# Early combine scores computed token-major, with the queries as the stationary side, in a decoder layer kernel

## The chip, the cores and the metric

The kernel runs on one core of a Trainium2 chip. The metric is the device time of one execution in microseconds (us), as the median of several runs. Three runs of the kernel before gave 1522.98, 1519.18 and 1523.01 us. Shorter is better.

## What is computed

One decoder layer on x of shape (2, 2048, 512) in fp32: a state-space mixer, a cross-attention to 77 context tokens and a soft mixture of 16 experts, each with a residual and a layer norm behind it. The last part is the one that matters here. Sixteen slots attend to all tokens (dispatch), each expert works on its slot, and the tokens then attend to the slots (combine), with 16 heads of 32 features:

```python
o = q + _mha(q, x, x, d_Wq, d_bq, ...)             # slots gather from tokens
h = _layernorm(os, e_ln_g, e_ln_b)
u = silu(h @ e_W1 + e_b1); g = silu(h @ e_Wg + e_bg)   # one expert per slot
o = o + ((u * g) @ e_W2 + e_b2)
out = _mha(x, o, o, c_Wq, c_bq, ...)               # tokens gather from slots
# in _mha: scores = einsum(qh, kh) / sqrt(32); softmax over the keys
x = _layernorm(x + out)
```

The combine's softmax runs over 16 slots for each of 4096 tokens and 16 heads.

## The kernel before

The kernel has four stages: in-projection and scan, token mixing with cross-attention and dispatch, the experts, and the combine. The first two end near 930 us and the change doesn't touch them.

**Experts** (`expert`, L1159). The 16 experts run one after the other on 32 rows (2 sequences, 16 slots). The weights of an expert are 12 MB, in 12 blocks of 1 MB: four of `e_W1`, four of `e_Wg`, four of `e_W2`. SP issues their loads in order, into a ring of slabs (`weights`, L1047); a load waits until PE has read what its slab held. PE multiplies a block of W1 or Wg into `up`; the block's 512 columns go to four column strips of 32. At k = 0 the bias is added by four more products with `bb`. ACT takes Silu of `up` into `sv`, DVE multiplies the two into `ag`, PE transposes `ag` into `tp` (L1181, PSUM tag `tr`), DVE copies the expert's columns into `aT` (L1185), and PE adds the four W2 blocks into `yac` (L1189).

**Work beside the experts.** While the weights of experts 2 to 13 stream, PE computes the combine's queries `Qc`, features on the partitions (`queries`, L1214). Behind expert 13 the slots of the first 14 experts are final: `slots_now`, `slot_heads` and `by_heads` (L1265 to L1292) make their keys and lay them out block-diagonally over the four heads of a group in `bd["c_Wk"]` (in the trace `c_Wkd`).

**Early scores** (`early`, L1315). The scores of all tokens against the 14 finished slots are computed while experts 14 and 15 run. A group g has 512 tokens, and there are 8 groups. In a group, PE makes the scores with the slots on the partitions (L1325, stationary `c_Wkd`, 64 columns, moving 512 query columns) into two PSUM tiles `lp` (in the trace `mm`), ACT copies them to `es`, and PE transposes them in pieces of 128 tokens into `sc` (L1333, in the trace `tr<-cst,es`), so that tokens are on the partitions. For each half group (256 tokens) DVE takes the maximum (L1338), subtracts it (L1339), ACT takes the exponential (L1341), and DVE sums (L1342). The result stays in `p`, one tile for each half group.

**What sets their order.** `early` is a generator. `beat` (L1149) is called behind each of the 12 weight blocks of experts 14 and 15, and takes the next steps from it; the steps are dealt over the first `b1` beats. What a beat takes may not be issued before the beat's last product. Steps that are left at the end are taken behind the last expert (L1350). Within these bounds a scheduler of the framework places the instructions in each engine's queue when the program is built. The PSUM tag `tr` has two buffers, shared by `sc`, `tp` and the transposes of the queries.

**Combine** (L1360 on). The last slots are completed (`slots_now` into `ysb`, `yp`, `oT`), their keys and values made (`fo`, `kr`, `ftr`, `bdl`), the scores of the last two slots added (`fsc`), the weights scaled (`factors`, `attend`), multiplied by values and output weights (`finish`), normed and stored.

Of the kernel before, what the change touches and what calls it, by code (L numbers as in the profile page):

```python
# [25 lines left out]
# columns of the packed per-partition vectors  # L26
# [3 lines left out]
# columns of the packed shape constants  # L30
# [34 lines left out]
def merge(*flows):  # L65
    """Emit flows side by side, each given as (generator, steps), at the pace that ends them together."""
    todo = [[f, n, 0] for f, n in flows]
    while todo:
        f = min(todo, key=lambda t: t[2] / t[1])
        f[2] += 1  # L70
        try:
            next(f[0])
        except StopIteration:
            todo.remove(f)


def weave(flows, depth, lag):
    """Emit `depth` flows side by side; the next one starts `lag` steps after the last."""
    flows = list(flows)
    live, since = [], lag  # L80
    while flows or live:
        if flows and len(live) < depth and (since >= lag or not live):
            live.append(flows.pop(0))
            since = 0
        since += 1
        for f in list(live):
            try:
                next(f)
            except StopIteration:
                live.remove(f)  # L90
# [123 lines left out]
 'b1': 18,  # L214
# [9 lines left out]
def tile_decoder(ctx, tc, a, out, dbg=None, upto=9, opt=None):  # L224
# [68 lines left out]
    with ExitStack() as st:  # L293
        class Pools:
            """tiles by tag from pools of their own, so that the next phase takes over each pool's room as it falls free"""
# [33 lines left out]
        def first_operands():  # L329
            """the first tokens and the weights in the order of their use, in pieces"""  # L330
            xt = sb.tile([128, 4, TB], FP, tag="xt", bufs=1, name="xt")
            xh = sb.tile([128, 4, TB], FR, tag="xh", bufs=2, name="xh")
            xl = sb.tile([128, 4, TB], FR, tag="xl", bufs=2, name="xl")
            nc.sync.dma_start(xt, a["xT"][0][:, 0:TB].rearrange("(k p) t -> p k t", p=128))
            wr = {}
            for q in (1, 0, 2):
                wr[q] = big_tile("wr", [128, 4, D], "CS" if q == 0 else "BS")
                for k in (0, 2):
                    nc.sync.dma_start(wr[q][:, k:k + 2, :], rows_of("wi")[:, k:k + 2, q * D:q * D + D])
            nc.sync.dma_start(cst, a["cst"])  # L340
            for k in (0, 2):
                split(xh[:, k:k + 2], xl[:, k:k + 2], xt[:, k:k + 2])
            x0.extend((xh, xl))
            for q in (1, 0, 2):
                for k in range(4):
                    split(wi[q][0][:, k, :], wi[q][1][:, k, :], wr[q][:, k, :], engs[EA.get("fl%d%d" % (q, k), 1)], EA.get("fh%d%d" % (q, k), 0))
                    if q != 1 and k % 2:
                        ready_.add(("wi", q, k))
                        yield
                if q == 1:  # L350
                    yield

        # decay: dt, cumulative sums, normalisers in rows (section of 512 tokens, head)
# [59 lines left out]
        def setup():  # L413
            """operands of the next phase from weights, a half at a time"""
# [5 lines left out]
            # cross-attention keys and values  # L420
# [32 lines left out]
            # dispatch queries folded with the key weights  # L453
# [91 lines left out]
        def scan_loads(c):  # L545
            """operands of one pass that holds the three hi/lo products of the 32 state rows"""
            scr = cvs[c // 2][1]
            sl = slice((c % 2) * 128, (c % 2) * 128 + 128)
            BS = big_tile("BS", [128, 4, 4, 128], "BS", FR)
            CS = big_tile("CS", [128, 4, 4, 128], "CS", FR)  # L550
            for q in range(3):
                dq = slice(32 * q, 32 * q + 32)
                for t, nm, j in ((BS, "Bc", q % 2), (CS, "C", q // 2)):
                    (nc.sync, nc.scalar)[EA.get("bq" if nm == "Bc" else "cq", 0)].dma_start(t[dq].rearrange("p g r t -> p (g r) t").bitcast(FP),
                                      scr[nm][j][:, sl].rearrange("(h n) t -> n h t", n=32).bitcast(FP))
            return BS, CS
# [3 lines left out]
        def scan_ready(c):  # L560
            """token-major x (weighted) and B of a chunk"""
# [79 lines left out]
        def next_weights():  # L641
            """weights of the next phase, into the room that the in-projection's leave"""
# [8 lines left out]
        def spread(*flows):  # L651
            """names side by side, each given as (name, steps), at the pace that ends them together"""
            return "".join(n for _, _, n in sorted(((k + 1) / n, i, c) for i, (c, n) in enumerate(flows) for k in range(n)))
# [30 lines left out]
    def stats(pool_, z, p=128, tg=""):  # L684
        """mean and 1/std over the free axis of z [p, 512]; the latter from exp(-ln(var+eps)/2) and a Newton step"""
# [13 lines left out]
    with ExitStack() as st:  # L699
# [222 lines left out]
        # Two half periods of four quarters for every tile; a stage works on the tile `back` periods ago.  # L922
        # Each quarter holds one group of heads of the attention and one block of products.
# [5 lines left out]
        def period(p):  # L929
            """operations of one period, in the order of their issue"""  # L930
# [86 lines left out]
    if True:  # L1017
# [17 lines left out]
        # the combine's weights stay in the slabs 0, 1, 2: the keys' come before the last experts', the others after  # L1035
# [34 lines left out]
        # sums over the tokens, divided by the sums of the weights, with their features on the partitions  # L1070
# [20 lines left out]
        # the slots after the dispatch and their norm; feature 4p+j sits on partition p  # L1091
# [17 lines left out]
        def mean(v):  # L1109
            """mean over the features, on all partitions"""  # L1110
            part = sb.tile([128, 32], FP, tag="part", bufs=2, name="part")
            dve.tensor_reduce(part, v.rearrange("p j b s -> p (b s) j"), AX.X, ALU.add)
            mp = ps.tile([128, 32], FP, tag="mm", bufs=2, name="mp")
            mm(mp, mean_w, part, True, True)
            return mp
# [27 lines left out]
    Qc = []  # L1143
    if True:
# [4 lines left out]
        def beat(e, at):  # L1149
            """scores of the tokens in the waits for the last expert's weights"""  # L1150
            if e >= NE - NL:
                n = tail["n"] = tail.get("n", -1) + 1
                b0, b1 = opt.get("b0", 0), opt.get("b1", 22)
                k = [max(0, min(1, (i - b0) / (b1 - b0))) * 3 * NT for i in (n, n + 1)]
# [101 lines left out]
        # what the slots hold besides the experts' sums  # L1256
# [8 lines left out]
        def slots_now(on):  # L1265
            """the slots with what the experts gave so far"""
# [8 lines left out]
        def slot_heads(nm, on, PS, pool_, tags=("kr0", "kr1")):  # L1275
            """keys or values of the slots without their bias, features on the partitions"""
# [11 lines left out]
        def by_heads(dst, src, cv, n):  # L1288
            """block-diagonal over the heads of a group"""
# [14 lines left out]
        esp = ctx.enter_context(tc.tile_pool(name="es", bufs=1, side="left", reuse_waits="tile"))  # L1304
# [10 lines left out]
        def early():  # L1315
            """the scores of all slots but the last experts': maxima, exponentials and their sums"""
            for g in range(B * NT // 2):
# [3 lines left out]
                es = [esp.tile([128, 512], FP, tag=f"es{m}", bufs=1, name="es") for m in range(2)]  # L1321
                for m in range(2):
                    lp = PE_("mm", (128, 512))
                    for q in range(2):
                        mm(lp[64 * q:64 * q + 64, :], bd["c_Wk"][:, 2 * m + q, b].rearrange("p r s -> p (r s)"),  # L1325
                           Qc[b][:, 2 * m + q, t0:t0 + 512], True, True)
                    cp(opt.get("ese%d" % m, 0), es[m], lp)
                yield
                for h in range(2):
                    sc = PE_("tr", (128, 2, 16, 16))  # L1330
                    for t in range(2):
                        for m in range(2):
                            pe.transpose(sc[:, t, 8 * m:8 * m + 8, :].rearrange("p h s -> p (h s)"),  # L1333
                                         es[m][:, (2 * h + t) * 128:(2 * h + t) * 128 + 128], ident)
# [26 lines left out]
    with ExitStack() as st:  # L1361
# [18 lines left out]
        def slot_outputs(b, m):  # L1380
            """values of the slots times the output weights for two groups of heads"""
# [4 lines left out]
        def split_outputs(b, m):  # L1386
            vp = vps.pop((b, m))
            if m == 0:
                # the weights of a head sum to one, so that its rows carry the output bias
# [3 lines left out]
        # keys of the last slots, each group of heads on the first columns of a strip  # L1393
# [12 lines left out]
        def last_slots(g):  # L1406
            """scores of 512 tokens for the last slots"""
# [8 lines left out]
        def factors(g):  # L1416
            """factors for the weights of the other slots, and the weights of the last ones"""
# [175 lines left out]
```

## Time and profile before

| What | us |
|---|---|
| Time, median of 3 runs (lowest, highest) | 1522.98 (1519.18, 1523.01) |
| Span of the profiled execution | 1526.7 |
| PE, DVE, ACT, POOL busy in it | 1372.1, 905.6, 616.3, 446.2 |
| First to last early score product (`mm`, `tr`) | 1378.9 to 1421.5 |
| Last `yac` products | 1428.4 to 1434.3 |
| First scores of the last slots (`fsc`) | 1440.1 |
| Combine behind them, to the end | 1441 to 1526.7 |

The profiled execution is 3.7 us longer than the median of the runs. The page has 40 slices of 38 us; the part that the change touches, 1379 to 1441 us, lies in slices 37 and 38, counted from 1. In the table by stage DVE is busy for 53.5 us of the 56.8 us from 1441.2 to 1498.0, and for 32.4 of the 62.2 us from 1379.0 to 1441.2. An instruction's row names the tile that it writes and those that it reads; a product of fp32 tiles shows twice, once for each of its two passes.

### The profile page before, as it was taken

Reading aid. Unit: us, or ns where it says so; the run is one execution under the profiler, and the core shown is the slowest. Engines: PE = TensorE matmul, PEld = TensorE weight load, DVE = VectorE, ACT = ScalarE, POOL = GpSimd, SP = SyncE. Lnnn points to the kernel's source line nnn. Section 1 sums busy time; section 2 is a strip of 40 time slices with the busy share of each in tenths; the row PEclk is TensorE's granted clock in tenths of the full one; section 3 lists DMA queues with packets and bytes.
Section 4 is the critical chain, followed back from the end, with each engine's and each line's share of the span. In section 5 each row is a group of like instructions: output and inputs, shape, how many; then the busy total and the mean of one; then the engine's idle time right before and its main releaser. Section 6 shows DMA issues by size and latency. Waiting matters only on the chain.

```text
span 1526.7 us, 27382 instructions
## 1 busy us (share of the span) xinstructions
PE 1372.1 (90%) x10282; PEld 996.3 (65%) x10282; DVE 905.6 (59%) x2142; ACT 616.3 (40%) x1683; POOL 446.2 (29%) x496
## 2 busy tenths in 40 slices
PE   7899999978999999999999997948979788889896
PEld 5788889857888888888888875205544445433364
DVE  6897796856788888888888764001211111115597
ACT  5544443524565565665656552001000000104456
POOL 3644543535444444444443321000000000000054
PEclk9999998988999999999999998969989998999998
DMA  9797987895122221311110138898999999999447
GB/s 312 194 214 206 227 219 194 223 248 143 56 56 60 66 63 57 96 57 56 57 53 18 70 139 350 355 415 359 418 419 418 420 419 419 418 421 408 174 149 251
DMA packets 177499, 339.61 MB, mean 222 GB/s; under 512 B 12027, under 2 KB 123131, under 8 KB 152536
## 3 DMA queue, kind: packets, MB, share of 16 engines
q1 hardware_dynamic: 161072, 311.25, 58.5%
q10 hardware_dynamic: 16296, 26.62, 5.1%
q8 instruction: 81, 1.33, 0.4%
q14 instruction: 50, 0.41, 0.1%
HBM read 299.56 MB, written 38.27 MB: 221 GB/s over the span
## 4 chain that ended last, share of the span: by engine, by line
PE 60%; DVE 17%; DMA 15%; ACT 4%; issue 3%; SPq 1%; POOL 1%; ACTq 0%; POOLq 0%; DVEq 0%
PE mm L231 25%; DMA ew<-in_e_W 8%; PE pj L231 7%; PE up L231 7%; DMA ew<-in_e_Wg 5%; PE tr L826 3%; PE yac L231 2%; PE sc L231 2%; PE y L231 2%; PE dps L231 2%; PE uu L231 2%; PE gp L231 1%; DVE X L528 1%; ACT pp L816 1%; PE tr L719 1%
## 5 line engine op out<-in xcount | busy, mean ns | idle before, releaser
L231 PE MATMUL up<-ew,hT 128*32 128x512 f32 x944 | 134.7, 645 | 34.4 <-DMA ew<-in_e_W 30.9
L818 POOL TENSOR_TENSOR pp<-pp,den 128x308 f32<-128x308 f32 x128 | 90.1, 708 | 161.4 <-DVE den L817 109.0
L1174 ACT ACTIVATE sv<-up 128x512 f32<-128x512 f32 x32 | 19.1, 597 | 269.8 <-PE up L231 247.0
L1183 POOL MEMSET aT<- 128x512 f32 x16 | 8.3, 524 | 403.5 <-PE yac L231 401.8
L231 PE MATMUL mm<-xTh,cqh 128*128 128x256 f32 x256 | 76.2, 309 | 26.2 <-ACT xTh L234 26.2
L1233 DVE TENSOR_TENSOR Qc<-mm,vec 128x512 f32<-128x512 f32 x32 | 22.1, 691 | 125.3 <-PE mm L231 125.3
L242 DVE TENSOR_TENSOR xTl<-tr,xTh 128x512 fp32r<-128x512 f32 x32 | 21.3, 687 | 115.1 <-ACT xTh L234 115.0
L231 PEld LDWEIGHTS up<-ew,hT 128*32 128x32 f32 x944 | 26.0, 112 | 96.6 <-issue 56.7
L826 PE MATMUL tr<-cst,pp 128*77 128x128 f32 x512 | 80.6, 282 | 1.4 <-ACT pt L234 1.2
L231 PE MATMUL mm<-x1Th,w30h 128*128 128x256 f32 x256 | 76.9, 301 | 4.4 <-DVE ql L786 3.6
L816 ACT ACTIVATE pp<-sc,mx 128x77 f32<-128x77 f32 x240 | 75.4, 327 | 13.3 <-DVE mx L813 12.5
L234 ACT COPY pt<-tr 77x512 f32<-77x512 f32 x96 | 55.7, 582 | 61.2 <-PE tr L826 34.2
L231 PE MATMUL mm<-xTl,cqh 128*128 128x256 f32 x256 | 78.4, 308 | 1.2 <-DVE xTl L242 1.2
L231 PEld LDWEIGHTS mm<-xTh,cqh 128*128 128x128 f32 x256 | 51.5, 207 | 40.2 <-ACT xTh L234 30.2
L231 PE MATMUL mm<-xTh,cql 128*128 128x256 f32 x256 | 75.2, 296 | 0.0
L231 PE MATMUL mm<-x1Tl,w30h 128*128 128x256 f32 x256 | 74.4, 291 | 0.9 <-DVE x1Tl L722 0.9
L231 PE MATMUL mm<-x1Th,w30l 128*128 128x256 f32 x256 | 73.8, 288 | 0.0
L826 PEld LDWEIGHTS tr<-cst,pp 128*77 128x77 f32 x512 | 59.4, 148 | 16.3 <-issue 11.1
L234 ACT COPY raw<-pj 128x512 f32<-128x512 f32 x48 | 28.1, 584 | 99.1 <-PE pj L231 65.0
L231 PE MATMUL yac<-ew,aT 128*32 128x512 f32 x488 | 61.1, 637 | 7.1 <-issue 4.7
L744 POOL TENSOR_TENSOR ut<-ut,fb 128x512 f32<-128x512 f32 x32 | 41.0, 1282 | 80.4 <-DMA ut<-Ud 40.9
L231 PEld LDWEIGHTS mm<-xTl,cqh 128*128 128x128 f32 x256 | 52.3, 204 | 18.4 <-issue 14.7
(376 smaller groups left out, 4358.1 us busy)
## 6 DMA issues: line engine op xcount, KB each, us to landing
ew<-in_e_W SPq DMA_DIRECT2D x119, 1024.0 KB, 15.9
ew<-in_e_Wg SPq DMA_DIRECT2D x60, 1024.0 KB, 14.1
BS<-scrBc SPq DMA_DIRECT2D x48, 256.0 KB, 5.7
CS<-scrC SPq DMA_DIRECT2D x48, 256.0 KB, 6.2
xt<-in_x SPq DMA_DIRECT2D x32, 256.0 KB, 2.8
ut<-Ud SPq DMA_DIRECT2D x32, 256.0 KB, 3.4
fb<-fd SPq DMA_DIRECT2D x128, 64.0 KB, 3.0
x2d<-x ACTq DMA_DIRECT2D x32, 256.0 KB, 2.0
```

Source lines behind the costliest of these rows:

```text
L231: return pe.matmul(o, lhsT=l, rhs=r, start=start, stop=stop, **kw)
L234: (act.copy, dve.tensor_copy, pool.tensor_copy)[e](o, i)
L242: (lo_eng or dve).tensor_tensor(lo, src, hi, ALU.subtract)
L528: dve.scalar_tensor_tensor(dst, raw[:, j, 1 + t:1 + t + TB], w4[:, t:t + 1], dst, ALU.mult, ALU.add)
L719: pe.transpose(tp[:, k * 128:k * 128 + 128], src[:, k * 128:k * 128 + 128], ident)
L744: (act, dve, pool)[EN.get('uf', 1)].tensor_tensor(ut, ut, fb, ALU.mult)
L816: act.activation(pp[:, r, :], sv[:, r, :], AF.Exp, bias=mx[:, h:h + 1], accum_out=den[:, h:h + 1])
L818: (act, dve, pool)[EN.get('d%d' % hg, 2)].tensor_tensor(pp, pp, den[:, h4].unsqueeze(2).to_broadcast([128, 4, S]), ALU.mult)
L826: pe.transpose(tp[0:S, r * 128:r * 128 + 128], pp[:, r, :], ident)
L1174: last["silu"] = act.activation(sv, up, AF.Silu)
L1183: pool.memset(aT, 0.0)
L1233: dve.tensor_tensor(Qc[b][:, mp * 2:mp * 2 + 2, t1:t1 + TB], qq, vec[:, V_CQ + mp * 2:V_CQ + mp * 2 + 2].unsqueeze(2).to_broadcast([128, 2 ...
```

## The change

In `early` the products change sides. The queries of 128 tokens are now the stationary operand and the block-diagonal keys of a head group, 64 columns, the moving one, so that the scores come out with tokens on the partitions, straight into `sc`. The tiles `lp` and `es`, the ACT copies and the transposes go, and so does the pool of `es`. The four operations behind the scores stay as they are.

A group now yields behind each block of 128 tokens and behind each half group, six times, where it yielded three times. `beat` deals 4 x 8 = 32 steps where it dealt 3 x 8 = 24, over 15 beats where it had 18. Docstrings and comments of the kernel are blanked, and the lines behind `early` have numbers smaller by six.

```diff
- 'b1': 18,
+ 'b1': 15,
...
-                k = [max(0, min(1, (i - b0) / (b1 - b0))) * 3 * NT for i in (n, n + 1)]
+                k = [max(0, min(1, (i - b0) / (b1 - b0))) * 4 * NT for i in (n, n + 1)]
...
-        esp = ctx.enter_context(tc.tile_pool(name="es", bufs=1, side="left", reuse_waits="tile"))
         xrp = ctx.enter_context(tc.tile_pool(name="xrp", bufs=1, side="left", reuse_waits="tile"))
...
-                es = [esp.tile([128, 512], FP, tag=f"es{m}", bufs=1, name="es") for m in range(2)]
-                for m in range(2):
-                    lp = PE_("mm", (128, 512))
-                    for q in range(2):
-                        mm(lp[64 * q:64 * q + 64, :], bd["c_Wk"][:, 2 * m + q, b].rearrange("p r s -> p (r s)"),
-                           Qc[b][:, 2 * m + q, t0:t0 + 512], True, True)
-                    cp(opt.get("ese%d" % m, 0), es[m], lp)
-                yield
                 for h in range(2):
                     sc = PE_("tr", (128, 2, 16, 16))
                     for t in range(2):
-                        for m in range(2):
-                            pe.transpose(sc[:, t, 8 * m:8 * m + 8, :].rearrange("p h s -> p (h s)"),
-                                         es[m][:, (2 * h + t) * 128:(2 * h + t) * 128 + 128], ident)
+                        for hg in range(4):
+                            mm(sc[:, t, 4 * hg:4 * hg + 4, :].rearrange("p r s -> p (r s)"),
+                               Qc[b][:, hg, t0 + (2 * h + t) * 128:t0 + (2 * h + t) * 128 + 128],
+                               bd["c_Wk"][:, hg, b].rearrange("p r s -> p (r s)"), True, True)
+                        yield
```

## The prediction, made before the change was run

> **What bounds the kernel now.** The granted-clock row of the page first: full speed nearly everywhere, so stages can be compared. Then the chain of waits from 1360 us on, because the order of instructions in the two built programs is the same on every engine until the first early score, at 1378.9 us, and again from the combine's first products (`fo`) on. Start and length in us, engine, line:
>
> ```profile
> 1395.86 0.63 PE tp L1181 x4
> 1396.49 0.69 issue
> 1397.18 1.07 PE yac L231 x8
> 1398.24 1.02 PE tr L1333 x8
> 1399.27 1.00 PE yac L231 x8
> 1400.26 1.87 PE mm L231 x8
> ...
> 1424.09 1.28 ACT L1174
> 1425.39 0.61 ACT sv L1174
> 1426.02 0.70 DVE ag L1178
> 1426.85 1.09 PE tp L1181 x4
> 1427.94 0.47 issue
> 1428.41 5.83 PE yac L231 x32
> ```
>
> PE is the bound from 1397 to 1423.4: weights (`up`, `yac`) and scores (`mm`, `tr`) alternate without a hole. Then a Silu table load, Silu, a product and a transpose lead to the last `yac`. In the table by stage the DMA share is 0.98 in 1423.4-1428.4 and 0.07 after: the stream ends near 1429, and as two other matrices (c_Wv, c_Wo; 1 MB each, 2.5 us at 415 GB/s) come behind the last expert's, its own are in by about 1425. DMA is 3 us off the bound. Now the groups that go, and the row nearest to what comes (busy us, mean ns | idle before):
>
> ```profile
> L231 PE MATMUL mm<-Qc,c_Wkd 128*64 128x512 f32 x64 | 16.4, 611 | 0.0
> L1333 PE MATMUL tr<-cst,es 128*128 128x128 f32 x64 | 9.8, 284 | 0.0
> ...
> L231 PE MATMUL kp<-qbd,dwk 128*128 128x64 f32 x32 | 3.9, 271 | 0.0
> ```
>
> The third has the new shape exactly: 128-column stationary side, 64 moving columns, fp32 in two passes, 3.9/32 = 0.122 us a pass; inside a run passes start 0.112 us apart.
>
> Last, stretches of 3.41 us, the step in which the clock changes here (PE, PEld, DVE, ACT, POOL busy, then clock):
>
> ```profile
> 258.62:262.03 3.41, 3.41 (x32) 3.41 (x32) 1.88 (x9) 2.48 (x5) 0.38 (x2) 1.00 0.90 278
> 262.03:265.44 3.41, 3.41 (x19) 3.41 (x17) 2.52 (x6) 0.00 (x0) 1.31 (x1) 0.50 1.02 275
> ...
> 1391.84:1395.25 3.41, 1.70 (x9) 0.61 (x8) 1.92 (x4) 3.37 (x6) 0.00 (x0) 1.00 1.01 420
> ...
> 1422.56:1425.97 3.41, 0.83 (x8) 0.00 (x0) 2.05 (x4) 2.98 (x4) 0.00 (x0) 1.00 0.99 415
> 1425.97:1429.39 3.42, 2.06 (x12) 1.10 (x16) 0.96 (x3) 1.30 (x2) 0.00 (x0) 0.50 0.81 308
> ```
>
> The first row matters most: PE was busy all of it, and yet the next stretch ran at half clock. Half of it was this:
>
> ```profile
> 258.78 1.85 PE L231 MATMUL qp<-sqTs,dwq 128*128 128x16 f32 x16
> ```
>
> 16-column passes wait for their weight loads; the array hardly streams. So what the clock follows looks like streamed columns, not busy time.
>
> **The change part by part.** *Products.* Per 512 tokens, four 512-column products (1.87 us in the chain) and eight transposes (1.02) go, 2.9 us, times 8 = 23.1 us of PE. In come 128 products of two passes: a half-block of 256 tokens (8 products) is 16 x 0.112 = 1.79, with the 0.16 us that a change of kind costs (the eight transposes take 1.02 where 8 x 0.109 = 0.87) 1.95 us, times 16 = 31 us. PE work grows by 8 us; it can't shrink unless a pass undercuts its weight load, which no row shows.
>
> *Copies.* Sixteen ACT copies of 0.58 us go (9.3 us). ACT is idle as long again in the stretch, so worth 0, except that products no longer wait for them. DVE's three operations and ACT's exponential per half-block stay. Pool `es` goes and `xrp` moves; SP's and POOL's orders are unchanged, one early wait less on SP near 990 us: 0.
>
> *Beats.* A group of 512 tokens now has 6 steps, 48 in all, but 32 are spread over 15 beats. So 22 of 32 token blocks are issued in the beats and 10 (5 half-blocks) are flushed behind the last expert. In the built order 8 products stand between its transposes and `yac`, 7 between its four weight blocks, 9 behind them and 16 between `yp` and `fo`.
>
> *Sum at full clock.* I lay the new order out with 1.0 us per weight block, 1.86 with its bias, 1.05 / 1.95 / 3.7 for 4 / 8 / 16 products. From 1378.9: 16 products to 1382.6, then block, 8, block, 8, block to 1389.5, 16 to 1393.2. The transposes `tp` need the PSUM buffer of the fifth half-block, whose subtraction stands on DVE behind `ag` and a sum that waits for an exponential behind Silu and a table load: 1390.3 + 1.28 + 0.6 + 0.6 + 1.15 = 1393.9. `aT` is now behind two more DVE operations, to 1395.4. So `yac` starts at 1395.5 (1397.2 before), PE standing 0.7 + 1.0 us. Then 15 us of the old blocks and 8.8 us of products end the last `up` near 1419.3 (1423.4 before): 4 us won, all weights in. The Silu table is loaded ahead, so `tp` follows after 1.5 us instead of 3.5. `yac` with its interleaved products ends at 1429.4 (1434.3). There DVE takes over: from `ysb` four half-blocks of 1.7-1.9 us, each with its exponential between subtraction and sum, hold `oT` and the first `kr` back to 1438.5 (1437.8), and the combine's `fsc` starts at 1441.2 against 1440.1. All 5 us are given back: **+1 us**. The combine is DVE-bound (53.5 of 56.8 us) in its old order and moves with it.
>
> *The clock.* An fp32 pass of 512 columns lasts 0.43 us, so 64 columns stream 0.053, half of the 0.112 us that the pass takes. Counting streamed time so (fp32r at half of that) over all stretches of 3.41 us at full clock: all 20 with a share up to 0.35 were followed by half clock, all from 0.46 up kept it, 0.38-0.45 went both ways. Of those at half clock, all up to 0.74 stayed and all from 0.78 came back. The score products alone are at 0.46-0.48: just on the safe side until PE stands. Around 1393 it does: 1.4 us of products at 0.46, `tp` (0.43), 1.7 us of nothing give 1.07/3.41 = 0.31; the luckiest position of the stretch gives 0.39. I take the fall.
>
> The rule that speaks against this is in the Trainium skill, TensorE: Matmul & The Clock Gate, "Why this matters for your kernels": the clock is lost only after gaps between matmuls above some 3 us. No gap here is above 1.5, so by the rule the price is 0 and the sum +1. By the row at 258.6, with no gap at all, it falls. I go by the row.
>
> At half clock a weight block takes 1.8 us and 4 / 8 products 2.0 / 3.9. Blocks and products by turns give 0.67-0.72, under the 0.78 that brings it back, until the last expert's first block with its bias (3.6 us of dense streaming). From 1395.5 to there 11.0 us become 20.5: **+9.5 us**. Behind it all moves by that. Then 9 products, the 32-column `yp` and 16 products stand in a row: 0.38, a second fall, whose 2.8 us of products and 1.9 of `fo` double, DVE hiding a part: **+2.5 us**. Sum 1 + 9.5 + 2.5 = 13 us.
>
> The page's span is 1526.7, so 1539.7 by it; the profiled execution lies 3.7 us over the median of 1522.98. On the median: **1536 us**.
>
> **The rivals.**
> - *Both falls, the second early* (0.27). The 1.5 us of idleness before the last `tp`, and the 8 sparse products behind it, share one stretch: 0.33-0.44. If it falls, `yac` and all 40 flushed products run at half clock to about 1461, and `fsc` starts near 1464: +24, 1547 us. For it: a stretch whose position is chance; against it: the dense blocks before.
> - *The clock holds* (0.17). PE idles less than I think near 1393, or the clock counts weight loads; decided by whether that stretch's share is above 0.45. Then +1: 1524 us, not slower. For it: 1391.84-1395.25 before had 0.38 by my count and kept full clock.
> - *Faster* (0.10). The clock holds, and DVE's four half-blocks fit beside `yac`, since PE's sparse products come sooner; the 4.9 us won at `yac` reach the combine: 1518 us. Against it: the built DVE order puts `oT` and `kr` behind them.
> - *That it does less than it says*: a third of the scores leave the waits that hide them; that is in all sums.
>
> **How the numbers follow.** Main case 0.46, both falls 0.27, holds 0.17, faster 0.10. Within 0.3% (4.6 us, about what a measurement can tell from no change) lie 0.16 of the holding case; the rest of it, a few us more of waits, goes to slower. Faster 0.10, same 0.16, slower 0.74. The range reaches from the holding case, less 2 us for the spread of the runs before, to the double fall plus 2: 1522 to 1549. It leaves out the faster case and the far ends of the others.
>
> **What would show it.** Right: half clock from about 1395 to 1416, passes of `tr<-c_Wkd,Qc` near 0.22 us there and 0.11 before; `up` of the last expert ending near 1429; `fsc` near 1453. The flush: `oT` behind a subtraction. Wrong: full clock in 1390-1420, or a start of `fsc` within 3 us of 1440; or a pass that costs other than 0.112 us at full clock.

## The result, and the profile after

The changed kernel takes 1542.03 us (median; 1536.25 to 1547.12), the kernel before beside it 1521.08 us: a ratio of 1.0125, 95% interval 1.0093 to 1.0157. The two medians lie 21 us apart; the ratio makes it some 19 us. The profiled execution of the changed kernel has a span of 1538.8 us, 12.1 more than that of before.

The chain of waits of the changed kernel, read from the first early score (1375.38 us here) to the first `fsc`:

```profile
1386.12 1.28 ACT L1174
...
1391.12 0.64 DVE p L1333
1391.89 1.09 PE tp L1181 x4
1393.45 1.94 PE yac L231 x8
1395.39 1.90 PE tr L231 x8
1397.29 1.87 PE yac L231 x8
...
1410.30 3.57 PE up L231 x16
...
1416.41 1.93 PE tr L231 x16
...
1426.66 1.28 ACT L1174
...
1429.42 0.63 PE tp L1181 x4
...
1446.18 0.64 DVE p L1333
...
1449.87 1.91 PE fsc L231 x8
```

The same eight passes of a weight block that took 1.00 to 1.07 us take 1.87 to 1.94 us here, and eight passes of score products take 1.90 us where the row at 1416.41 has 16 in 1.93. That is half speed from `tp` to the block at 1410.30. The hole ahead of `tp`, from PE's timeline (idle before, and its releaser):

```profile
1391.89 1.09 PE L1181 MATMUL tp<-cst,ag 128*128 128x128 f32 x4 [2.16 <-DVE p L1333]
```

The table by stage shows where it begins and ends (PE, PEld, DVE, ACT, POOL busy, granted clock, DMA share, GB/s):

```profile
1387.59:1391.00 3.41, 2.14 (x20) 2.00 (x18) 1.75 (x3) 2.29 (x3) 0.00 (x0) 1.00 1.01 416
1391.00:1394.41 3.41, 2.04 (x12) 0.95 (x12) 2.65 (x7) 1.08 (x2) 0.00 (x0) 0.50 1.01 420
1394.41:1397.83 3.42, 3.42 (x20) 1.98 (x16) 0.62 (x1) 0.07 (x1) 0.00 (x0) 0.50 1.01 422
...
1411.48:1414.89 3.41, 3.41 (x17) 1.29 (x10) 0.00 (x0) 0.00 (x0) 0.00 (x0) 0.50 0.48 118
1414.89:1418.30 3.41, 3.41 (x33) 2.44 (x33) 1.87 (x3) 0.58 (x1) 0.00 (x0) 1.00 0.71 235
```

In the first row PE stands for the first 1.3 us of this hole; the next stretch is at half clock, and although PE is busy for all of most stretches that follow, full clock returns only at 1414.89, after the last expert's first block with its bias (`up`, 1410.30, 512 columns a pass). A hole of this kind stands in the kernel before too, 2.32 us ahead of 1395.86, and there the clock was kept. By the prediction's count columns stream for 0.38 of that stretch, between its limits; the first row here comes to about 0.30 (some 19 passes of 0.053 us).

Counted from the first early score, the last `up` ends after 51.2 us (44.5 before), and `fsc` starts after 74.4 us (61.2 before): +13.2. From `fsc` to the end it is 89.0 us against 86.6: +2.4, with half clock from 1449.03 to 1455.85. The first score happened to come 3.5 us earlier in this execution. 13.2 + 2.4 - 3.5 = 12.1: from a common start, the change costs 15.6 us between these two executions.

### The profile page after: what moved, and what is told of

Read it like the earlier page. It is cut to its first block, busy times and chain, and to the rows that moved or that the text cites. A ratio compares the mean times of both kernels' runs of the same rounds, so it can differ in the third digit from the quotient of the medians.

```text
span 1538.8 us, 27609 instructions
## 1 busy us (share of the span) xinstructions
PE 1385.9 (90%) x10410; PEld 1020.7 (66%) x10410; DVE 910.2 (59%) x2142; ACT 608.6 (40%) x1667; POOL 447.6 (29%) x496
## 4 chain that ended last, share of the span: by engine, by line
PE 58%; DMA 18%; DVE 16%; ACT 4%; issue 2%; SPq 1%; POOL 1%; ACTq 0%; POOLq 0%; DVEq 0%
PE mm L231 23%; DMA ew<-in_e_W 9%; PE pj L231 7%; DMA ew<-in_e_Wg 6%; PE up L231 6%; PE tr L826 3%; PE yac L231 2%; PE y L231 2%; PE sc L231 2%; PE dps L231 2%; PE tr L231 2%; PE uu L231 1%; PE gp L231 1%; DVE X L528 1%; ACT pp L816 1%
```

## The experiments

Two theories stood at the start. *Clock*: passes of 64 columns stream too little to bring the clock back once a hole has taken it. *Flush and beats*: the 5 half-blocks left behind the last expert, and the shorter beats, delay the combine. The first four kernels set them against each other.

**Twice the columns, same passes** (changed kernel). The keys of both sequences (128 columns) move; the half that belongs to the other sequence is overwritten by the next product. For that, one of the eight products of a half-block stays at 64 columns, and the second sequence takes its products in reverse within a half-block. The number of passes, the beats and the flush stay.

```diff
-  mm(sc[:, t, 4 * hg:4 * hg + 4, :]..., Qc[b][...], bd["c_Wk"][:, hg, b]..., True, True)
+  mm(flat_[:, o_ - 64 * b:o_ - 64 * b + 128], q_, bd["c_Wk"][:, hg]..., True, True)
```

> The changed kernel with one edit: the moving side of a score product is 128 columns (both sequences' keys) where it was 64; the surplus half lands where the next product overwrites it, so the scores are the same. Number of products, weight loads, order and flush stay; only the streamed share of a pass goes from about 0.48 to 0.96. Theory (the clock follows streamed columns): no half clock between 1375 and 1440 us, passes 0.112 us apart, last `up` ends 44 to 46 us after the first score product (51 with the change), time 1.001 to 1.006 of before. Rival (the larger PE work and the flush behind the last expert cost the time, the clock is only a companion): still about 1.0125 of before.

1526.07 us, ratio 1.0028 [1.0012, 1.0044]. More streamed columns make the kernel faster by about 1%. The table by stage of this kernel, from the stretch with the hole on:

```profile
1381.66:1385.07 3.41, 1.25 (x12) 1.14 (x11) 2.17 (x5) 1.52 (x3) 0.00 (x0) 1.00 1.01 416
1385.07:1388.49 3.42, 2.95 (x13) 0.91 (x13) 2.26 (x6) 0.92 (x2) 0.00 (x0) 0.50 1.01 422
1388.49:1391.90 3.41, 3.41 (x16) 1.76 (x16) 0.00 (x0) 0.00 (x0) 0.00 (x0) 0.50 0.83 346
1391.90:1395.31 3.41, 3.41 (x31) 2.35 (x28) 1.44 (x3) 0.58 (x1) 0.00 (x0) 1.00 0.79 274
```

The hole is there, and the clock falls:

```profile
1384.95 0.98 PE L1181 MATMUL tp<-cst,ag 128*128 128x128 f32 x4 [2.17 <-DVE p L1338]
```

What differs is the way back: two stretches, not seven. I had expected the fall itself to be absent; the width decides the return.

**No flush** (changed kernel, 64 columns): all 48 steps inside the 15 beats.

```diff
-  k = [max(0, min(1, (i - b0) / (b1 - b0))) * 4 * NT for i in (n, n + 1)]
+  k = [max(0, min(1, (i - b0) / (b1 - b0))) * 6 * NT for i in (n, n + 1)]
```

> The changed kernel with one edit: 48 steps are dealt over the 15 beats where 32 were, so no score product is left behind the last expert. Flush theory: the tail is as before the change, time 0.998 to 1.004 of before. Clock theory: the fall near the third block of expert 14's W2 stays, with more sparse products beside the weights it lasts as long or longer, and only the 3 to 5 us of the flush come back: 1.007 to 1.013.

1542.78 us, ratio 1.0144 [1.0104, 1.0184]; half clock from 1380.90 to 1415.03. The flush is not what costs; the ratio is a little above the 1.007 to 1.013 of the clock theory, and the interval reaches into it.

**Both of these together.**

> Both edits: 128 moving columns and 48 steps in the beats. Clock theory: full clock throughout; PE carries 8 us more than before in its bound stretch, of which the holes near `tp` (2.3 us before) take some: 1.001 to 1.005 of before. Flush theory: as with the spread steps alone, 0.998 to 1.004. If the time is well above 1.005, the 8 us of weight loads are a cost of their own.

1530.94 us, ratio 1.0062 [1.0039, 1.0084], a little above what I expected. Nor is it at full clock throughout: its profile has one stretch of 3.41 us at half clock behind each of two holes, from 1382.05 and from 1423.01. That without the flush more of the added PE work lies in the stretch that PE bounds is my reading, not shown.

**The products by themselves.** Only fp32 products, the kernel's computation left out: 112 products of each width behind dense ones of 512 columns, then widths rising with nothing dense between.

```python
for n in FALL:                    # 64, 60, 56, 52, 48, 44, 40, 32, 16
    series("dense", 512, DENSE)
    series("f%d" % n, n, EACH)
for n in RISE:                    # 64, 80, 96, 104, 112, 120
    series("r%d" % n, n, EACH)
```

> This kernel leaves the whole computation out; it only runs series of fp32 products with a 128-column stationary side, each with its own weight load, and its time isn't compared. After 12 us of dense 512-column products come 112 products with 64, 60, 56, 52, 48, 44, 40, 32 and 16 moving columns, then without dense ones between 64, 80, 96, 104, 112 and 120. PE never stands. Streamed-column theory: at 64 and 60 (shares 0.48, 0.45) the clock holds, at 44 and below (0.33) it falls within 7 us, the limit lies between 0.36 and 0.43 (48 to 56 columns); from half clock it doesn't come back at 64, 80, 96 (0.72), and does at 112 (0.84), perhaps at 104 (0.78). Busy-time theory: full clock in all series.

The groups with shapes kept apart (busy us, mean ns | idle before); `f` follows dense products, `r` is the rise:

```profile
L32 PE MATMUL r<-mv,wt 128*128 128x80 f32 x224 | 48.0, 421 | 0.0
L32 PE MATMUL f<-mv,wt 128*128 128x48 f32 x224 | 42.9, 382 | 0.0
L32 PE MATMUL r<-mv,wt 128*128 128x96 f32 x224 | 27.7, 291 | 0.0
L32 PE MATMUL f<-mv,wt 128*128 128x64 f32 x224 | 25.1, 275 | 0.0
L32 PE MATMUL f<-mv,wt 128*128 128x52 f32 x224 | 25.1, 275 | 0.0
```

and the table by stage, inside `f` of 52, `f` of 48 and `r` of 80 columns (this kernel has no ACT column):

```profile
129.50:153.50 24.00, 24.00 (x217) 24.00 (x217) 0.52 (x1) 0.00 (x0) 1.00 0.01 1
174.00:208.00 34.00, 34.00 (x161) 34.00 (x161) 0.00 (x0) 0.00 (x0) 0.50 0.00 1
495.00:538.00 43.00, 43.00 (x204) 43.00 (x204) 0.00 (x0) 0.00 (x0) 0.50 0.00 0
```

PE and its weight loads are busy without a gap in all three rows. At full clock a group of 224 passes takes 25.1 us from 52 to 64 columns: the 0.112 us of a pass is set by the weight load, not the width. 52 columns keep the clock, 48 lose it; 64 and 80 stay at half clock for their whole 48 us each, 96 return to full within 5.3 us, which I had not expected. So 64 columns hold a full clock but can't win it back, and 96 can; 128 is not in the series. That is the difference between the two widths above, with no other work around.

A second set asked which part of the change carries the loss, and what a hole is needed for.

**Without the hole** (changed kernel, 64 columns): the scores take PSUM buffers that `tp` doesn't share.

```diff
-  sc = PE_("tr", (128, 2, 16, 16))
+  sc = PE_("mm", (128, 2, 16, 16))
```

> The changed kernel with one name changed: its score tiles take PSUM buffers that nothing else is waiting for, so the transposes tp of expert 14 no longer wait for the subtraction of the fifth half-block. The products stay 64 columns wide. Clock theory (a hole starts the fall, 64-column products can't bring it back; by the series of bare products, 64 columns alone keep the full clock): full clock from 1375 to about 1410 and one short fall behind the last expert's up as in every run; ratio to before 1.000 to 1.005. Rival, narrow products among other work are enough for the fall: half clock in 1390-1415 again, ratio 1.010 to 1.014.

1537.5 us, ratio 1.0098 [1.0061, 1.0136]: far from the 1.000 to 1.005 that I expected of the clock theory, next to the rival's 1.010. The timeline of PE shows why (start, length, what, idle before and its releaser):

```profile
1367.78 1.09 PE L231 MATMUL up<-ew,hT 128*32 128x512 f32 x8 [1.99 <-DMA ew<-in_e_Wg]
...
1397.23 1.06 PE L1181 MATMUL tp<-cst,ag 128*128 128x128 f32 x4
```

`tp` waits for nothing now, as wanted. But another hole, a wait for weights ahead of the first score, took the clock, and the narrow products kept it down for 51 us:

```profile
1368.70:1419.90 51.20, 50.59 (x227) 33.11 (x220) 15.35 (x27) 7.79 (x11) 0.00 (x0) 0.50 0.66 258
```

So a hole of another kind does the same. This is one execution, and one of the longer ones (1546.06 us). Over this kernel's seven runs the time goes with the mean clock: the shortest, 1526.97 us, has 0.952, the longest, 1549.04 us, 0.938. The part of the theory that named the hole at `tp` as the cause doesn't hold: it is one occasion among several.

**The beats alone** (kernel before, old products): `'b1': 18` to 15.

> The kernel before with its old products and copies, and only the end of the beats moved from 18 to 15 as in the change. If the beats carry the loss: 1.005 or more. Clock theory: the old products are 512 columns wide, the clock returns within one or two stretches of 3.41 us, ratio 0.998 to 1.003.

1530.08 us, ratio 1.0045 [1.0024, 1.0067], above the 0.998 to 1.003 that the clock theory expected, though the interval reaches into it. PE's timeline around expert 14's `tp`:

```profile
1389.08 0.63 PE L1333 MATMUL tr<-cst,es 128*128 128x128 f32 x4 [2.32 <-DVE p L1339]
1390.27 1.09 PE L1333 MATMUL tr<-cst,es 128*128 128x128 f32 x4 [0.56 <-DVE p L1339]
1392.91 1.09 PE L1181 MATMUL tp<-cst,ag 128*128 128x128 f32 x4 [1.56 <-DVE p L1339]
1395.00 1.93 PE L231 MATMUL yac<-ew,aT 128*32 128x512 f32 x8 [1.00 <-issue]
```

The same steps in fewer beats put PE three times behind DVE's subtraction, 4.4 us in all, and it stands for 1.00 us more ahead of `yac`: 5.4 us of idleness where the kernel before has 2.32 + 0.69. Half clock lasts from 1389.91 to 1400.15, three stretches where I had expected one or two.

**The products alone** (changed kernel, 64 columns): 48 steps over the old beats, `'b1': 18`, nothing flushed.

> The changed kernel with the beats as they were before: their end back at 18, and all 48 steps inside them, so no scores are left behind the last expert. The products are those of the change, 64 columns. Clock theory: the hole in front of tp or a wait for weights still comes, and from there blocks and narrow products by turns stay at half clock to the last expert's biased block: ratio 1.008 to 1.014, most of the change's loss without its beats. Rival, the beats and the flush carry the loss: 1.000 to 1.004.

Ratio 1.0127 [1.0085, 1.0168], with runs from 1536.87 to 1555.10 us: within this scatter, the whole loss of the change without its beats. PE waits 2.17 us for DVE's `p` at 1385.77, and half clock lasts from 1386.47 to 1417.19.

**In search of a better version.** 128 columns and the separate PSUM buffers, with 32 steps in 15 beats, with 48 in 15, and with 48 in 18; and 128 columns with 48 in 18 and the shared buffers:

> Both repairs of the changed kernel: 128 moving columns and PSUM buffers without the wait at tp. Clock theory: full clock from 1375 to the end of the last expert's up; 0.3% (the 128-column version) less the hole of some 2.6 us and the stretch or two of half clock behind it (up to 3 us): ratio 0.998 to 1.002, a draw with before. Rival, the 8 us of added weight loads in a stretch that PE bounds stay whole: 1.003 to 1.006.

> As the 128-column version without the wait, and all 48 steps inside the 15 beats, so nothing of the scores is left behind the last expert. If the flush costs anything once the clock holds, this is faster than the same with 32 steps: ratio 0.996 to 1.000. If PE's added weight loads bound the stretch wherever they lie: same as the other within 0.2%, 1.000 to 1.004.

> The same once more, with PSUM buffers without the wait at tp. If the hole at tp costs what its idle time says (2.6 us), 0.1 to 0.2% below the version with the wait: 0.997 to 1.002. If the experts' weights set the end of this stretch, the same as that one.

> The same old beats with the products at 128 columns. Clock theory: one or two stretches of half clock behind each hole, as before the change. The 0.45% that the beats alone cost with the old products goes, and the 8 us of PE work remain, partly hidden: ratio 0.998 to 1.003. If PE's added loads set the end: 1.004 to 1.006.

| 128 columns | Ratio, own PSUM buffers | Ratio, shared buffers |
|---|---|---|
| 32 steps in 15 beats | 1.0017 [0.9999, 1.0035] | 1.0028 [1.0012, 1.0044] |
| 48 steps in 15 beats | 1.0033 [1.0018, 1.0048] | 1.0062 [1.0039, 1.0084] |
| 48 steps in 18 beats | 1.0023 [1.0007, 1.0039] | 1.0062 [1.0042, 1.0082] |

None beats the kernel before. Spreading all steps did not gain over leaving some behind, against my hope. With own buffers and 48 steps in 18 beats the ratio is just above the 0.997 to 1.002 expected. With shared buffers and 48 steps in 18 beats I expected 0.998 to 1.003 and missed; the size is nearer to the other case, that PE's added loads set the end (1.004 to 1.006), but the same loads with own buffers give 1.0023. In the profiles: with shared buffers PE stands for 2.16 us and again for 1.52 ahead of `yac`, and one stretch of 3.41 us (1391.43 to 1394.85) runs at half clock; with own buffers it stands for 1.73 us and keeps its clock. That is 3.7 us (1.95 of idleness, 1.7 of clock) of the 6 us between the two. Behind the last expert the half clock lasts two stretches with shared buffers and one with own, and the last `yac` takes 5.87 us against 4.98; the rest is open. The last 0.2 to 0.3% were not taken apart further; the 8 us of added PE work are the first suspect, but that is argued only.

## Why the prediction was right, and which of its terms were off

- *PE work up by 8 us; ACT's copies, POOL and SP worth 0.* A pass starts every 0.112 us in the bare series from 52 to 64 columns, and 16 passes take 1.93 us in the kernel at full clock (1.95 predicted). At half clock 8 take 1.90 (2.0), 16 take 3.61 (3.9). That the copies were worth nothing was not tried by itself; the versions with 128 columns, at best 1.0017, leave no gain of theirs to see.
- *The beats.* The order was as predicted, and with narrow products the beats add nothing that the intervals would show (1.0125 with them, 1.0127 without). But by themselves, with the old products, they cost 0.45%; the prediction had no term for that.
- *The layout at full clock.* Here one step failed: "The Silu table is loaded ahead". The load waits for `up` and lies whole, 1.28 us, on the path, at both experts (1386.12 and 1426.66 in the chain). At expert 14 the sum has one table load, the exponential's; two stand one behind the other (1386.12 and 1388.03). From ACT's timeline:

```profile
1386.12 1.28 ACT L1174 ACT_TABLE_LOAD   x1 [2.10 <-PE up L231]
```

ACT had been idle for 2.10 us before it, and still the load didn't start. So the hole at `tp` is 2.16 us where 0.7 was predicted, and the last `tp` starts 2.9 us behind the last `up`, not 1.5. The two loads, 2.6 us, are about the difference between the 13 us of the sum and the 15.6 measured from the first score.

- *The fall.* Predicted 14 us behind the first score (1393), it is 15.6 us behind it (1391.00). From the first `yac` to the end of the biased block 20.5 us were predicted; 1393.45 to 1413.87 is 20.4. The last `up` ends 51.2 us behind the first score, 49.9 predicted: the 1.3 us are the table load. The rule weighed against this, that the clock is lost only after gaps above some 3 us (Trainium skill, TensorE: Matmul & The Clock Gate, "Why this matters for your kernels"), would have left +1 us of 19. The gap here is 2.16 us, and in the bare series, where the clock falls at 48 columns, there is none. With 128 columns and own buffers a gap of 3.11 us ahead of the first `yac` kept the clock.
- *DVE at the end.* From the last `yac` to `fsc` 11.8 us were predicted (5.9 before); 12.1 were measured.
- *The second fall.* Its size held (2.5 predicted, ahead of `fsc`; 2.4 lost behind it), its place didn't: the stretch with 9 products, `yp` and 16 products kept full clock, and the one in which PE waits for `kr` (1445.61 to 1449.03, PE busy for 2.36 of 3.42 us) lost it.
- *From the page to the median.* The span predicted was 1539.7 us; it is 1538.8. That closeness is in part luck: the two table loads made the change 2.6 us dearer than predicted, and the first score came 3.5 us early in this execution. Nor was the surplus of the profiled execution of before 3.7 us: that figure sets a span against a time, and in the runs on record the time is 1.8 to 2.2 us longer than the span. By an estimate from this, that execution took 1528.7 us, 5.7 above its median of 1522.98, while the changed kernel's took 1540.85 us, 1.2 below its own. With the 12.1 us between the two spans, that makes the 19 us. So of the 6 us between 1536 and 1542, 2.6 are the table loads. The cause of the other 3.4 stays open: the chance of two single executions, or a cost that these two profiles don't show.

Of the rivals, *the clock holds* (1524 us) is what 128 columns with their own PSUM buffers give: 1526.49 us, at full clock from 1370.5 on through the combine. The rival *both falls* was nearer than the result lets it seem. Half clock that begins within 1.1 us of the last `tp` stands in nine of the twelve profiles of whole kernels, the kernel before among them (from 1425.97 us, `tp` at 1426.85). But in none of the nine do 40 flushed products of 64 columns follow, and the clock is back after one or two stretches. The changed kernel's profile has the flush and not the fall, and its other three executions have no profile. Nothing shows *faster*.

## What to carry to other kernels

Before narrowing the moving side of a product, compare its columns with those that its weight load lasts for: when the load sets the pace, PE stays busy, but the array streams too little to get its clock back after the next hole, and every other product in the stretch pays. So look at the row of granted clock behind each hole, not only at the hole, and put something wide behind it. A profile of one execution has its own luck: count from an event that both profiles have, as the first score here, and set spans against spans and times against times.

## What the runs showed of the hardware

- Fall and return have different limits, with PE and its weight loads busy without a gap throughout: fp32 passes of 52 columns keep full clock and of 48 lose it; at half clock 80 columns stay and 96 return. In shares of the time in which columns stream: at full clock, with 0.43 us for 512 columns and 0.112 us a pass, 52 and 48 columns are 0.39 and 0.36. At half clock 512 columns take twice as long and a pass takes 0.214 us (48.0 us for 224), so 80 and 96 columns are 0.63 and about 0.75. Both pairs fit the limits read from the kernel before (0.35 to 0.46 down, 0.74 to 0.78 up); the 0.72 that was expected to stay at half clock came of using the full-clock pass.
- The fall at 48 columns was not immediate: full clock lasted from the start of the series at 166.16 us to 171.59, the end of the first step of 3.41 us that lies wholly in the series; the mean of these passes, 382 ns against 421 for a series wholly at half clock, shows the mixture.
- Widening a pass from 64 to 128 columns cost nothing that can be seen at full clock: 32 passes take 3.79 us at both widths.
